# Four gelus in one ScalarE block, or in two blocks of two

## The chip, the core and the metric

The kernel runs on one core of one Trainium2 chip. The core has five engines with queues of their own, each of which works strictly in order: PE (TensorE, matmuls), DVE (VectorE), ACT (ScalarE), POOL (GpSimd) and SP (SyncE, which here only issues DMAs). They wait for one another through semaphores. The metric is device time in microseconds (us). The kernel before takes 3993.9 us, the median of 3 runs (3993.34 to 3994.86).

## What is computed

The input is x, 8 images of 384 channels and 32 x 32 places, so 1024 tokens each. Layer 0 is a two-way state space scan beside a small convolution, layer 1 is attention and a feed-forward part with quantised activations. Cut to what matters:

```python
# layer 0
fwd = mamba(x_flat, ...); bwd = flip(mamba(flip(x_flat), ...))
#   mamba: in-projection, 4-tap convolution, silu, softplus, then for each token
#   h = exp(delta * A) * h + delta * u * B;  y = sum over 16 states of h * C
local = sigmoid(depthwise_3x3(x_norm)) * x_norm
x = x + res_scale * (scale_mod * (fwd + bwd) + local)
# layer 1
t = t + attention(layernorm(t))          # 6 heads, causal
h = layernorm(t) @ sign(W1 - mean) + b1  # 1536 wide
h = gelu(clip(h * 128 / max|h|))         # the maximum over one image
t = t + clip((h @ sign(W2 - mean) + b2) * 128 / max)
```

The reference quantises in five groups of images, and with eight images each group is one image. The three images beyond them get zero from the feed-forward part, so it runs for five of the eight images only.

## The kernel before

Everything is float32, with channels on the 128 partitions and tokens along the free dimension. The weights' signs, the scan's inputs and other intermediate results go through DRAM.

**The planner.** The kernel's functions do not issue instructions. They record operations (`Op`), and `Plan.place` (line 246) then lays them out in time: it simulates the five engines with a cost for each operation (`Plan.cost`, line 221; a table load counts 2.8 there), gives each free engine the ready operation of the lowest rank, and hands out tile buffers on the way. `Plan.emit` (line 357) issues the result, which is why nearly every row of the profile has line 367. A rank is the operation's number in the order of recording. `hurry(offset)` lowers it, so that the operation goes ahead of others that are ready. `together()` makes one operation out of several instructions, between which nothing else of that engine can stand. A change in one place can move operations everywhere behind it.

**The order of recording.** The functions hand their steps to lists with a weight each (`Steps.of`). `spread_over` (line 1512) mixes lists by these weights. In the main loop (lines 1586 to 1613) the attention of an image is followed by its feed-forward part, mixed with `before_scan` of the image that comes three later; in that mix a step whose weight is a `Gap` counts `SHORT` (3.0) instead, all times `JOINT` (0.6). The scan units of the next image are spread over all of it.

**The scan.** There are 768 scan units, 96 for an image. One unit (`s_first`, `s_scan`, `s_sum`, lines 997 to 1045) is a chain over four engines:

1. POOL multiplies delta * u by B into a tile `scan_g` (128x1024), the first multiplication. There are 6 buffers of `scan_g`.
2. ACT makes two exps into PSUM, `ps_da` (two buffers).
3. DVE runs two scans over `scan_g`, each with one `ps_da`.
4. In half of the units ACT copies the last column out, the carry copy (`scan_carry<-scan_g`).
5. POOL multiplies `scan_g` by C in place, the second multiplication. It overwrites what the carry copy reads, so it waits for it.
6. For each pair of units PE gathers the states into `ps_y` (four small matmuls), which frees two `scan_g` buffers. The seed (`ps_y<-scan_us`, ACT) fills `ps_y` before the first gather, and `scan_yt<-ps_y` empties it in between.

These operations are recorded with a hurry of 600.

**The feed-forward part** (`feed_forward`, line 1394): a layernorm; 24 matmul groups with W1, evacuated by ACT into four tiles `st["h", q]` (128x3072, `big_big`); `quant_scale` (line 1382: a maximum on DVE, a transpose on PE with `small_col`, another maximum, add and multiply, reciprocal) which gives `st["s1"]`; then the gelus over the four tiles in place, with that scale, and four clamps on DVE; then six matmul groups of 12 with W2 (lines 1448 to 1478), whose k runs over the four tiles in turn, and each load of W2 is one of `mid_mid`; a second `quant_scale`; and the output.

**Beside it** runs `before_scan` (line 649). Its pieces that are named later: the taps of the 3x3 convolution (`local`, line 732: 8 multiply-adds on DVE for each of two halves, so 16, into PSUM, with `big_big` and `const_vec`), the gates block (`gates`, line 860: three silus of 128x1024, two tanhs of 128x512 and a table load back, one `together` group with a hurry of 60), `project_parts` (line 754, matmuls with `wx`), and `deltas` (line 913: matmuls with `wdt`, then the softplus block, three softplus and a table load, one `together` group).

**Tables.** ACT holds one table of functions. The set `LOG_EXP` (exp, ln, copies) is the resting one, and each group that needs another ends with `preload_act_table_set(LOG_EXP)`; the load ahead of the group is put in by the compiler. So every such group costs two loads.

After the feed-forward part comes the next image's attention: the output projection (`wout`), a layernorm (`onesc`), Q and K (`big_big` by `big_big`), V (`wv`), then the softmax.

Of the kernel before, what the change touches and what calls it, by code (L numbers as in the profile page):

```python
# [12 lines left out]
AF = mybir.ActivationFunctionType  # L13
ALU = mybir.AluOpType
# [7 lines left out]
NC = C // P  # L22
# [9 lines left out]
NF = FF // P  # L32
# [3 lines left out]
QCLIP = QMAX - QEPS  # L36
# [15 lines left out]
LOG_EXP = "natural_log_exp_and_others"  # L52
# [108 lines left out]
class Plan:  # L161
# [15 lines left out]
    @contextmanager  # L177
    def together(self):
        self.group = []
        yield  # L180
        self.group = None

    @contextmanager
    def hurry(self, offset):
        self.sooner += offset
        yield
        self.sooner -= offset
# [193 lines left out]
def kernel(  # L381
# [21 lines left out]
    nc = plan = Plan(tc, homes)  # L403
    together, hurry = plan.together, plan.hurry
# [989 lines left out]
    def feed_forward(b, t, emit):  # L1394
        st = {}

        @emit
        def _():
            st["xn"] = t()
            st["mxh"] = small.tile([P, NF], F32, name=f"mxh_{b}", tag="mxh", bufs=1)  # L1400
            st["mxy"] = small.tile([P, NC], F32, name=f"mxy_{b}", tag="mxy", bufs=1)
# [33 lines left out]
            st["s1"] = quant_scale(st["mxh"], f"h_{b}")  # L1435


        @emit.of(Gap(16.0))
        def _():
            with hurry(offset=60):  # L1440
                with together():
                    for q in range(NF // NC):
                        nc.scalar.activation(st["h", q], st["h", q], AF.Gelu, scale=st["s1"])
                    nc.scalar.preload_act_table_set(LOG_EXP)
                for q in range(NF // NC):
                    nc.vector.tensor_scalar(st["h", q], st["h", q], QCLIP, None, ALU.min)

        for m in range(NC):
            for h in range(NH):
# [220 lines left out]
```

## Time and profile before

| what | value |
|---|---|
| median of 3 runs | 3993.9 us |
| the profiled execution | 3992.03 us |
| its span, first to last instruction | 3990.2 us |
| mean granted TensorE clock | 0.901 |
| DMA | 612 MB, 153 GB/s over the span |
| scan exps, 1536 of 128x512 | 690 ns each |
| scans on DVE, 768 and 768 of 128x512 | 1267 and 1207 ns each |
| clamps, 20 of 128x3072 | 2325 ns each |
| taps on DVE, 128x496 | 732 ns each |
| silus of 128x1024, tanhs of 128x512 | 1046 and 644 ns each |

The five feed-forward parts' gelus begin at 1010.5, 1556.9, 2100.0, 2631.1 and 3156.2 us of the span. They are called blocks 1 to 5 below.

A row of a group shows line, engine, operation, output tile and input tiles without buffer numbers, shapes and count; then the total busy time, the mean of one in ns, and behind the second bar the time that the engine stood idle just before these instructions, with what ended it. A matmul of the program shows as two records. Busy times of matmuls are modelled at their ends, and so a PE that is busy is not at its peak.

### The profile page before, as it was taken

How to read it: one execution, taken by the hardware profiler on the slowest of the kernel's cores; microseconds unless marked ns; L12 is line 12 of the kernel's file. 1: busy time of each engine (PE TensorE's matmuls, PEld its weight loads, DVE VectorE, ACT ScalarE, POOL GpSimd, SP SyncE). 2: the span in 40 equal slices, each digit the busy share in tenths (PEclk: the TensorE clock that was granted, in tenths of full speed). 3: DMA queues.
4: the chain of work that ended last, by engine and by line, in shares of the span. 5: the costliest groups of instructions: out<-in, count | busy, mean ns of one | idle time of the engine just before them, and what ended most of it. 6: DMA issues, size and time to landing. Idle time of an engine off the chain costs nothing. (4 is left out here: it accounts for less than half of the span.)

```text
span 3990.2 us, 43097 instructions
## 1 busy us (share of the span) xinstructions
PE 3390.6 (85%) x12428; PEld 1334.1 (33%) x12428; DVE 3197.7 (80%) x4481; ACT 2627.6 (66%) x5114; POOL 3574.2 (90%) x1559
## 2 busy tenths in 40 slices
PE   5585779897799896998987989879989699898999
PEld 1131224332234332333322433323433234333344
DVE  5898987789878799788897688986779967878743
ACT  5767676866747777558677387674776746847635
POOL 2999999999999999999998799988999879999910
PEclk8695879999799997899987999979999799999999
DMA  7547664235543344742346433366334473333300
GB/s 246 195 157 247 230 239 133 90 132 186 194 170 123 117 157 149 250 151 93 127 162 224 157 122 113 130 202 237 104 111 136 157 252 128 111 123 114 121 14 32
DMA packets 338967, 612.01 MB, mean 153 GB/s; under 512 B 34616, under 2 KB 93416, under 8 KB 338728
## 3 DMA queue, kind: packets, MB, share of 16 engines
q1 hardware_dynamic: 329072, 593.10, 44.1%
q10 hardware_dynamic: 9656, 16.15, 1.2%
q8 instruction: 98, 1.61, 0.2%
q14 instruction: 141, 1.16, 0.1%
HBM read 456.03 MB, written 153.09 MB: 153 GB/s over the span
## 5 line engine op out<-in xcount | busy, mean ns | idle before, releaser
L367 POOL TENSOR_TENSOR scan_g<-scan_ud,scan_bc 128x1024 f32<-128x1024 f32 x768 | 1822.5, 2377 | 126.4 <-DMA scan_ud<-dram_sp_ud 62.6
L367 POOL TENSOR_TENSOR scan_g<-scan_g,scan_bc 128x1024 f32<-128x1024 f32 x768 | 1820.0, 2373 | 101.2 <-ACT scan_carry L367 55.5
L367 ACT ACTIVATE ps_da<-scan_dl,const_amat 128x512 f32<-128x512 f32 x1536 | 1053.4, 690 | 710.0 <-DVE scan_g L367 696.9
L367 DVE TENSOR_TENSOR_SCAN scan_g<-ps_da,scan_carry,scan_g 128x512 f32<-128x512 f32 x768 | 940.3, 1267 | 143.4 <-POOL scan_g L367 108.8
L367 PE MATMUL ps_any<-big_big,mid_mid 128*128 128x512 f32 x2016 | 956.8, 626 | 88.1 <-DVE big_big L367 64.8
L367 DVE TENSOR_TENSOR_SCAN scan_g<-ps_da,scan_g 128x512 f32<-128x512 f32 x768 | 895.9, 1207 | 153.7 <-POOL scan_g L367 98.3
L367 PE MATMUL ps_y<-scan_g,const_gather 128*32 128x512 f32 x3072 | 463.1, 679 | 236.7 <-POOL scan_g L367 232.3
L367 PEld LDWEIGHTS ps_any<-big_big,mid_mid 128*128 128x128 f32 x2016 | 389.0, 199 | 673.9 <-issue 491.1
L367 PE MATMUL ps_any<-big_big,big_big 128*128 128x512 f32 (+4 forms) x1728 | 548.0, 559 | 14.4 <-DVE big_big L367 5.6
L367 PE MATMUL ps_any<-const_ident,mid_mid 128*128 128x128 f32 x1728 | 311.5, 306 | 76.7 <-ACT mid_mid L367 45.3
L367 DVE CUSTOM_DVE_ANT_0 mid_mid<-ps_any,const_cmask 128x512 f32<-128x512 f32 (+3 forms) x576 | 292.0, 547 | 72.0 <-PE ps_any L367 71.6
L367 PEld LDWEIGHTS ps_any<-big_big,big_big 64*128 64x128 f32 (+1 forms) x1728 | 224.3, 191 | 303.1 <-issue 206.9
L367 DVE SCALAR_TENSOR_TENSOR ps_any<-big_big,const_vec,ps_any 128x496 f32<-128x496 f32 (+6 forms) x420 | 303.0, 727 | 16.4 <-ACT ps_any L367 6.6
L367 PEld LDWEIGHTS ps_any<-const_ident,mid_mid 128*128 128x128 f32 x1728 | 199.8, 150 | 309.3 <-issue 94.6
L367 ACT COPY ptp_ptn<-ps_any 128x512 f32<-128x512 f32 (+3 forms) x576 | 256.2, 479 | 49.0 <-PE ps_any L367 41.8
L367 PE MATMUL ps_any<-ptp_ptn,big_big 128*64 128x512 f32 (+3 forms) x1152 | 263.3, 537 | 13.8 <-ACT ptp_ptn L367 12.8
L367 ACT ACTIVATE mid_mid<-mid_mid,small_low 128x512 f32<-128x512 f32 (+3 forms) x384 | 242.5, 634 | 46.9 <-DVE small_low L367 46.6
L367 PEld LDWEIGHTS ps_y<-scan_g,const_gather 128*32 128x32 f32 x3072 | 63.2, 113 | 515.0 <-POOL scan_g L367 413.8
L367 ACT ACT_TABLE_LOAD x131 | 168.1, 1283 | 2.9 <-PEq L1657 0.7
L367 PE MATMUL ps_any<-mid_mid,const_onesc 128*128 128x512 f32 x252 | 130.2, 651 | 42.7 <-ACT mid_mid L367 27.5
L367 PE MATMUL ps_any<-mid_mid,const_wdt 25*128 25x512 f32 x192 | 139.0, 891 | 29.8 <-DVE mid_mid L367 15.9
L367 ACT COPY mid_mid<-ps_any 128x512 f32<-128x512 f32 x234 | 130.0, 584 | 35.9 <-PE ps_any L367 31.3
(102 smaller groups left out, 3136.3 us busy)
## 6 DMA issues: line engine op xcount, KB each, us to landing
scan_dl<-dram_sp_dl SPq DMA_DIRECT2D x384, 256.0 KB, 3.3
scan_ud<-dram_sp_ud SPq DMA_DIRECT2D x384, 256.0 KB, 3.9
scan_bc<-dram_rows SPq DMA_DIRECT2D x256, 256.0 KB, 3.4
scan_us<-dram_sp_u SPq DMA_DIRECT2D x96, 256.0 KB, 2.9
mid_mid<-dram_sp_u SPq DMA_DIRECT2D x96, 256.0 KB, 5.0
dram_sp_dl<-mid_mid SPq DMA_DIRECT2D x96, 256.0 KB, 4.6
dram_sp_ud<-mid_mid SPq DMA_DIRECT2D x96, 256.0 KB, 4.9
dram_sp_u<-mid_mid SPq DMA_DIRECT2D x42, 512.0 KB, 4.9
```

What stands on the lines that cost most here:

```text
L367: getattr(engine, what)(*[mapped(v) for v in args], **{k: mapped(v) for k, v in kwargs.items()})
```

## The change

The gelus of one feed-forward part are recorded as two steps, each with a group of two gelus and a load of the resting table, and with the two clamps that belong to them. The weights of the steps are 8 and 8 instead of 16 in the mix with `before_scan`; as each is a `Gap`, they count 3.0 each in the main loop, where one step counted 3.0 before.

```diff
-        @emit.of(Gap(16.0))
-        def _():
-            with hurry(offset=60):
-                with together():
-                    for q in range(NF // NC):
-                        nc.scalar.activation(st["h", q], st["h", q], AF.Gelu, scale=st["s1"])
-                    nc.scalar.preload_act_table_set(LOG_EXP)
-                for q in range(NF // NC):
-                    nc.vector.tensor_scalar(st["h", q], st["h", q], QCLIP, None, ALU.min)
+        for q0 in range(0, NF // NC, 2):
+
+            @emit.of(Gap(8.0))
+            def _(q0=q0):
+                with hurry(offset=60):
+                    with together():
+                        for q in range(q0, q0 + 2):
+                            nc.scalar.activation(st["h", q], st["h", q], AF.Gelu, scale=st["s1"])
+                        nc.scalar.preload_act_table_set(LOG_EXP)
+                    for q in range(q0, q0 + 2):
+                        nc.vector.tensor_scalar(st["h", q], st["h", q], QCLIP, None, ALU.min)
```

`NF // NC` is 4. The rest of the code is the same. The order in which the planner puts the instructions of all engines differs from a little ahead of the first gelu block on.

## The prediction

> **What bounds the kernel now.** The page's totals and its 40 slices come first, then its groups.
>
> ```profile
> PE 3390.6 (85%) x12428; PEld 1334.1 (33%) x12428; DVE 3197.7 (80%) x4481; ACT 2627.6 (66%) x5114; POOL 3574.2 (90%) x1559
> POOL 2999999999999999999998799988999879999910
> L367 POOL TENSOR_TENSOR scan_g<-scan_ud,scan_bc 128x1024 f32<-128x1024 f32 x768 | 1822.5, 2377 | 126.4 <-DMA scan_ud<-dram_sp_ud 62.6 <-PE ps_y L367 55.7 <-issue 8.0
> L367 POOL TENSOR_TENSOR scan_g<-scan_g,scan_bc 128x1024 f32<-128x1024 f32 x768 | 1820.0, 2373 | 101.2 <-ACT scan_carry L367 55.5 <-DVE scan_g L367 40.6 <-POOL scan_g L367 1.9
> L367 ACT ACT_TABLE_LOAD x131 | 168.1, 1283 | 2.9 <-PEq L1657 0.7
> L367 ACT ACTIVATE big_big<-big_big,small_qs 128x3072 f32<-128x3072 f32 x20 | 55.5, 2844 | 0.1
> ```
>
> POOL is full from the second slice to the 38th: each of 768 scan units takes two multiplications, 2.38 + 2.37 us. The chain of waits covers only the tail after POOL's last instruction (3% of the span), so it says nothing here. What matters is where POOL pauses: idle 126.4 + 101.2 us, of which 62.6 is the start, and most of the rest lies in stretches that begin at a block of gelus. Slices 22 and 23, 27 and 28, 32 and 33 (about 100 us each) show three of them. I then read the five blocks (tables loaded at 1009.2, 1555.6, 2098.7, 2629.8, 3154.9) in the timeline. The third:
>
> ```profile
> 2098.71 1.28 ACT L367 ACT_TABLE_LOAD   x1
> 2100.00 11.09 ACT L367 ACTIVATE big_big<-big_big,small_qs 128x3072 f32<-128x3072 f32 x4
> 2111.11 2.57 ACT L367 ACT_TABLE_LOAD   x2
> 2117.77 1.28 ACT L367 ACT_TABLE_LOAD   x1
> ...
> 2106.94 6.99 POOL L367 TENSOR_TENSOR scan_g<-scan_ud,scan_bc 128x1024 f32<-128x1024 f32 x3
> 2123.60 4.78 POOL L367 TENSOR_TENSOR scan_g<-scan_g,scan_bc 128x1024 f32<-128x1024 f32 x2 [9.66 <-DVE scan_g L367]
> ...
> 2101.67 9.83 DVE L367 SCALAR_TENSOR_TENSOR ps_any<-big_big,const_vec,ps_any 128x496 f32<-128x496 f32 x13
> 2111.41 9.14 DVE L367 TENSOR_SCALAR big_big<-big_big 128x3072 f32<-128x3072 f32 x4
> ...
> 2115.60 12.28 PE L367 MATMUL ps_any<-big_big,mid_mid 128*128 128x512 f32 x24 [11.25 <-DVE big_big L367]
> 2192.74 20.87 PE L367 MATMUL ps_any<-big_big,mid_mid 128*128 128x512 f32 x48
> 2214.72 13.94 POOL L367 TENSOR_TENSOR scan_g<-scan_ud,scan_bc 128x1024 f32<-128x1024 f32 x6 [7.57 <-PE ps_y L367]
> ...
> 2090.00:2310.00 220.00, 193.90 (x566) 76.88 (x568) 163.31 (x208) 120.93 (x198) 177.82 (x78) 0.88 0.56 189
> ```
>
> Each timeline line is start, length, engine, operation, tiles. The gelus and the gates block (silus, tanhs) behind them hold ACT from 2098.71 to 2119.05 with no scan exp between. POOL runs out of scanned tiles at 2113.94 and loses 9.66 us. PE waits too: the clamp that feeds the second weight matrix's matmuls (W2) stands on DVE behind 13 convolution taps. From 2115.60 to about 2300 PE hardly stops, and POOL pauses because its tiles are not gathered: 7.57 us behind 24 matmuls (48 records, 0.87 us a matmul). In the last line (window, then busy PE, PEld, DVE, ACT, POOL) PE is busier than POOL. So blocks 3 to 5 are bound by ACT for 10 us, then by PE. In blocks 1 and 2 PE isn't full; POOL loses 3.88 + 2.17 and 4.07 + 2.52 us there.
>
> **The change, part by part.** The gelus (20 x 2844 ns), the 20 clamps and all DMAs stay in number and size. Added are ten table loads, two in each of five blocks: 10 x 1283 ns = 12.8 us of ACT, which has 34% of the span free. A block of 1.28 + 11.10 + 1.28 = 13.7 us becomes two of 1.28 + 5.55 + 1.28 = 8.1. What stands between them is in the order of the changed program, read against the order before:
>
> - Blocks 1 and 2: one scan unit (a carry copy, two exps) between the halves and one between the second half and the gates.
> - Block 3: only a 0.6 us copy, then a seed of y. Block 4: nothing. Block 5: the gates come between the halves, and a softplus block that stood 8 units after the gelus now stands one unit after them.
>
> So ACT's longest stretch without a scan exp falls from 13.7 to 8.1 us in blocks 1 and 2, and grows in the others: 20.4 to 24.1 us (block 3: two loads 2.6, and the copy and the seed, which stood ahead), 20.4 to 22.9 (4 and 5).
>
> Block 1: the halves start about one unit earlier, since the quantiser's reciprocal no longer stands behind a scan pair on DVE. One unit is scanned 5 us later, the next 0.8 earlier: 8.1 + 1.5 + 8.1 + 1.5 + 6.7 = 25.9 us against 13.7 + 1.5 + 6.7 = 21.9 started about 4.7 later. Bounds: -3.9 (its first stall gone) and +2.6 (two loads on the path). I take -1, near the middle.
> Block 2: likewise, and three clamps (7.22 us) no longer stand together ahead of the scans at 1583.75. Bounds -6.6 and +2.6; I take -2.
> Block 3: on DVE the first clamp now stands ahead of the last four taps, so W2 may start 4 x 0.73 = 2.9 us sooner. Counted in PE's order over the 16 pairs of gathers behind the gelus, six V matmuls (0.66 us each) move out of them: 4.0 us less ahead of POOL. Against that, POOL's next scanned tile comes 2.6 us later; the gather that wants it is reached by PE some 1.4 us after that, so most of the delay is covered by PE's matmuls. Without this cover it costs up to 3.7. Bounds -6.9 and +3.7; I take -5.
> Block 4: three taps, 2.2 us, and one V matmul, 0.7. Scans 2.6 us later, covered by about 1.5 us. Bounds -2.9 and +2.6; I take -3, on the PE side, since PE is the bound there for 180 us.
> Block 5: no tap moves, PE's work ahead of POOL is the same over these pairs. Two clamps and two sums now stand ahead of a scan, and the softplus (4.3 us) comes early. Bounds 0 (hidden, as PE is busy from 3171.8) and 2.6 + 4.3 = +6.9; I take +3.
>
> Sum: -1 - 2 - 5 - 3 + 3 = -8 us; of the bounds, -20.3 and +18.4. Behind each block the planner orders other work anew; between these stretches POOL idles only 2 to 5 us in 310 to 430, so little is to be won there. The profiled run took 3992.03 us (3990.2 of span, 1.8 around), 1.9 under the median; its span should come to 3982 and the median to 3993.9 - 8 = 3986 us.
>
> The row of the loads shows 1283 ns, and the gelu begins 0.01 us after. The Trainium skill (ScalarE: Activation LUTs, What ACT_TABLE_LOAD costs) gives the same load and a drain of some 1380 ns with each switch; by it ten switches would be an estimated 26.6 us, not 12.8, and with all of them on the path 4020, not 4007. The trace shows no such gap behind a load.
>
> **Rivals.**
>
> *The loads are paid on the path (slower).* Three of the five splits have no scan between the halves, so the stall of 9.66 us in block 3 (8.79 and 5.36 in 4 and 5) grows by the loads. If POOL's tile at the end of the gates comes later than PE reaches its gather, PE stops as well, and the earlier W2 start is worth nothing. It decides from 1.4 us of lateness. Price: all ten loads, 12.8 us, 4007 us. For it: 20.4 to 24.1 us on ACT. Against: PE's 11 us wait at that place is for DVE, not ACT. The rule in the Trainium skill (ScalarE: Activation LUTs, Rules for kernel authors) to group by table set before switching speaks for this case.
>
> *The long matmul runs break up (much faster).* In the changed order the longest runs of W2 matmuls between two gathers are 21, 15 and 17 where they were 24, 29 and 34. The stalls behind them were 7.57, 7.72 and 10.17. Three matmuls less give back 2.6, and in blocks 4 and 5 the whole, 7.7 + 10.2: 20 us, 3974 us. Against: PE has as much to do altogether, and other runs grow (the 20 us run of block 5 behind the output projection).
>
> *Nothing moves (same).* POOL's gap only changes place: later scans in blocks 3 to 5 against fewer waits in 1 and 2; 3994 us.
>
> That the change does not do what it says is part of the first: in block 4 two table loads stand back to back between the halves.
>
> **How the numbers follow.** A measurement here tells about 0.2%, 8 us, from no change. The forecast gets 0.42 (0.22 beyond -8, 0.17 within, 0.03 slower), the loads on the path 0.33 (0.31 slower, 0.02 within), the broken runs 0.14, nothing 0.11 (all within). Faster 0.36, same 0.30, slower 0.34. The likeliest case's own range is 3979 to 3994. Together the range is 3973 (all lower bounds) to 4010, just under all upper bounds.
>
> **What would show it.** 141 table loads. In blocks 1 and 2 POOL's idle time near the gelus falls below 6.0 and 6.6 us. In block 3 W2 starts some 16 us after the first load or sooner, POOL's wait right at the gates is 11 to 13 us, and the idle time after it is shorter by more than that grows. In block 5 the first three second multiplications are spread wider by about 4 us. I am wrong if PE waits for POOL right after W2 starts, if POOL's idle time between 2090 and 2310 grows beyond today's 42 us, or if the attention stages, where POOL hardly stops now, begin to show pauses.

## The result, and the profile after

The changed kernel takes 3983.99 us (median of 9 runs, 3981.79 to 3985.73). The kernel before took 3994.34 us beside it (9 runs, 3990.76 to 3999.45). The ratio is 0.9974, with a 95% interval from 0.9966 to 0.9982: 10.4 us less, 0.26%. The profiled execution took 3981.79 us and its span is 3979.9 us, 10.3 less than before.

From the page of the changed kernel: the busy totals, POOL's 40 slices, POOL's two groups and the table loads.

```profile
PE 3393.5 (85%) x12428; PEld 1334.4 (34%) x12428; DVE 3196.9 (80%) x4483; ACT 2639.9 (66%) x5122; POOL 3577.6 (90%) x1559
POOL 2999999999999999999997899989999798999910
L367 POOL TENSOR_TENSOR scan_g<-scan_ud,scan_bc 128x1024 f32<-128x1024 f32 x768 | 1825.9, 2381 | 115.2 <-DMA scan_ud<-dram_sp_ud 62.8
L367 POOL TENSOR_TENSOR scan_g<-scan_g,scan_bc 128x1024 f32<-128x1024 f32 x768 | 1821.7, 2375 | 95.6 <-ACT scan_carry L367 71.8
L367 ACT ACT_TABLE_LOAD x141 | 180.9, 1283 | 3.1 <-PEq L1659 0.7
```

The ten loads are there (131 became 141, 12.8 us), and ACT is busy 12.3 us longer. POOL makes the same multiplications, and its idle time fell from 126.4 + 101.2 to 115.2 + 95.6 us, so by 16.8; but the two groups are busy 5.1 us longer (the last section shows how a multiplication can stretch). Its pauses still lie about the blocks, at slices 22, 23, 27, 32 and 34.

The third block in the timeline of the changed kernel (start, length, engine, operation, tiles, count, idle time before):

```profile
2092.11 1.28 ACT L367 ACT_TABLE_LOAD   x1
...
2093.41 5.60 ACT L367 ACTIVATE big_big<-big_big,small_qs 128x3072 f32<-128x3072 f32 x2
...
2099.48 2.34 POOL L367 TENSOR_TENSOR scan_g<-scan_ud,scan_bc 128x1024 f32<-128x1024 f32 x1
...
2102.22 5.60 ACT L367 ACTIVATE big_big<-big_big,small_qs 128x3072 f32<-128x3072 f32 x2
2102.74 3.42 DVE L367 TENSOR_SCALAR big_big<-big_big 128x3072 f32<-128x3072 f32 x2
2104.54 7.99 PE L367 MATMUL ps_any<-big_big,mid_mid 128*128 128x512 f32 x12 [14.64 <-DVE big_big L367]
...
2112.47 1.06 PE L367 MATMUL ps_y<-scan_g,const_gather 128*32 128x512 f32 x8
...
2113.71 4.66 POOL L367 TENSOR_TENSOR scan_g<-scan_ud,scan_bc 128x1024 f32<-128x1024 f32 x2 [11.89 <-PE ps_y L367]
```

W2 now starts 12.4 us after the first load (2104.54 against 2092.11); it was 16.9. POOL's pause at the gates grew from 9.66 to 11.89 us. What came after it shrank. The 7.57 us behind the long W2 run are gone; within the run (21 matmuls now) POOL pauses 2.80 us, and within the output projection 4.12 us, where it was 1.72. The pauses behind Q, K and V went from 3.44 + 7.34 + 2.99 to 5.47. The window from 2090 to 2310 us of the changed kernel shows the sum (busy us of PE, PEld, DVE, ACT, POOL):

```profile
2090.00:2310.00 220.00, 198.81 (x617) 78.66 (x617) 166.57 (x221) 131.34 (x221) 184.17 (x81) 0.91 0.57 193
```

POOL is idle 35.8 us in it, where it was 42.2.

To place gains I use 48 marks: the copies `scan_yt<-ps_y` on ACT, one for every 16 scan units. Six of them lie in smooth stretches between the blocks (the 12th, 19th, 26th, 33rd, 40th and 48th, at 766.7, 1489.2, 1983.5, 2508.6, 3028.7 and 3590.2 us in the kernel before). How much sooner or later a kernel reaches them gives the share of each stretch. For the changed kernel: +0.8 up to the first, then -3.0 (block 1), -4.0 (2), -7.8 (3), -0.1 (4), +1.7 (5), and +2.0 to the end of the span. These come from one execution of each kernel, and stretches with the same instructions in the same order still differ by up to 1, so only steps beyond that are read.

### The profile page after: what moved, and what is told of

Read it like the earlier page. It is cut to its first block, busy times and chain, and to the rows that moved or that the text cites. A ratio compares the mean times of both kernels' runs of the same rounds, so it can differ in the third digit from the quotient of the medians.

```text
span 3979.9 us, 43074 instructions
## 1 busy us (share of the span) xinstructions
PE 3393.5 (85%) x12428; PEld 1334.4 (34%) x12428; DVE 3196.9 (80%) x4483; ACT 2639.9 (66%) x5122; POOL 3577.6 (90%) x1559
## 3 DMA queue, kind: packets, MB, share of 16 engines
q8 instruction: 98, 1.61, 0.2%
## 5 line engine op out<-in xcount | busy, mean ns | idle before, releaser
L367 POOL TENSOR_TENSOR scan_g<-scan_ud,scan_bc 128x1024 f32<-128x1024 f32 x768 | 1825.9, 2381 | 115.2 <-DMA scan_ud<-dram_sp_ud 62.8
L367 POOL TENSOR_TENSOR scan_g<-scan_g,scan_bc 128x1024 f32<-128x1024 f32 x768 | 1821.7, 2375 | 95.6 <-ACT scan_carry L367 71.8
L367 PE MATMUL ps_any<-ptp_ptn,big_big 128*64 128x512 f32 (+3 forms) x1152 | 265.5, 541 | 14.6 <-ACT ptp_ptn L367 13.6
L367 ACT ACT_TABLE_LOAD x141 | 180.9, 1283 | 3.1 <-PEq L1659 0.7
L367 PE MATMUL ps_any<-mid_mid,const_wdt 25*128 25x512 f32 x192 | 134.7, 871 | 33.2 <-DVE mid_mid L367 16.7
L367 DVE COPY big_big<-ps_any 128x512 f32<-128x512 f32 (+1 forms) x85 | 53.8, 633 | 132.4 <-PE ps_any L367 132.1
```

Source lines behind the costliest of these rows:

```text
L367: getattr(engine, what)(*[mapped(v) for v in args], **{k: mapped(v) for k, v in kwargs.items()})
```

## The experiments

All times below are medians, beside runs of the kernel before on the same chip (3993.9 us in the first and third group, 3994.6 in the second). The first expectations speak of a gain by POOL's progress. That count misjoined some rows in blocks 4 and 5; the marks, each a single instruction, replace its +2.7 and +2.4 by -0.1 and +1.7.

### Splitting only some of the images

```diff
-        for q0 in range(0, NF // NC, 2):
+        nq = 2 if b in ORDER[:2] else 4      # split_01; split_234: b in ORDER[2:]
+        for q0 in range(0, NF // NC, nq):
...
-            @emit.of(Gap(8.0))
+            @emit.of(Gap(4.0 * nq))
```

> The feed-forward parts of images 0 and 1 are split as in the changed kernel, those of images 2, 3 and 4 keep one block of four gelus. POOL's progress (the time at which it begins its n-th multiplication) gained 3.0 us on the kernel before at the first block of the changed kernel, 3.7 at the second, 7.7 at the third, and lost 2.7 and 2.4 at the fourth and fifth. Theory A (each split acts in its own stretch; in the first two the gain is that ACT can make scan exps between the halves): the first two gains stay, 3994 - 6.7 = 3987 us, and the progress shows nothing of its own at blocks 3 to 5. Theory B (the gain is the earlier start of the matmuls with W2, so of the later blocks): some 3993 us. Theory C (the planner's new order behind the change decides, and the places of gain are chance): gains and losses of several us turn up at blocks 3 to 5 although they are as before.

> The reverse: images 2, 3 and 4 are split, 0 and 1 keep one block of four. Theory A: -7.7 + 2.7 + 2.4 = -2.6 and up to 1.7 at the end, 3990 to 3992 us, and POOL's progress up to 2000 us is that of the kernel before. Theory B: most of the gain of the changed kernel, 3986 us. Theory C: the sizes at blocks 3 to 5 are others than in the changed kernel, by more than 3 us at each.

With images 0 and 1 split: 3983.91 us (11 runs), ratio 0.9977 [0.9969, 0.9986], as fast as the changed kernel. With images 2 to 4 split: 3997.38 us (11 runs), 1.0007 [0.9998, 1.0016], no gain. The first keeps the gains of its split blocks, 2.8 and 2.9 us. But most of its change lies where it isn't split: block 3, which has its four gelus in one block as before, gained 12.5 us, and blocks 4 and 5 lost 5.3 and 2.8. In the second kernel the halves of block 3 stand on ACT as in the changed kernel, with loads and one copy between, and W2 starts 12.7 us after the first load, nearly as early as in the changed kernel (12.4), yet the block gains 1.1 instead of 7.8. What differs is around them: the seed of `ps_y` comes behind the gates, not ahead of them (POOL's pause there is 16.68 us, not 11.89), and 18 V matmuls stand between two gathers, not 14. So the time in blocks 3 to 5 does not follow from how they are split. Theory C, the order, was the only one of the three that both runs allow.

### The loads alone, newly planned

```diff
                     for q in range(NF // NC):
+                        if q == 2:
+                            nc.scalar.preload_act_table_set(LOG_EXP)
                         nc.scalar.activation(st["h", q], st["h", q], AF.Gelu, scale=st["s1"])
```

> The four gelus stay one block, with a table load to and from between the second and third: the ten loads of the changed kernel without a place for other work. Theory A: the 2.6 us are on POOL's path in blocks 1 and 2, where ACT's block ends its wait (+2.6 each), and in 3 to 5 half covered by PE's long runs (+1.2 each, by the 1.4 us of cover in the prediction): +9, 4003 us. Theory D (all loads paid): +12.8, 4007 us. Theory E (ACT has 34% of its time free, the loads are hidden): 3994 us.

4008.5 us (5 runs), 1.0038 [1.0025, 1.0051]: +14.6, more than all ten loads (12.8). Theory D is nearest, but the stretches don't fit it: +5.5, +2.5, +8.2, +2.2, 0.0, where two loads are 2.6 each. The planner had made a new order here too, so this run couldn't price the loads.

### Clamps behind their own gelus

```diff
+        if what == "activation" and self.group:
+            op.done_at[id(written[0].tile)] = op.time
...
-                [b.end + (0.0 if b.name == op.name and not b.dma else self.SIGNAL) for b in op.before.values()],
+                [
+                    b.start + b.done_at[id(op.tiles[0])] + self.SIGNAL
+                    if op.parts[0][0] == "tensor_scalar" and id(op.tiles[0]) in b.done_at
+                    else b.end + (0.0 if b.name == op.name and not b.dma else self.SIGNAL)
+                    for b in op.before.values()
+                ],
```

> No split and no added load: four gelus in one block, but the planner is told when each gelu of the block ends, so that each clamp may be placed behind its own gelu and not behind the whole block. On DVE the clamps now stand one by one among the last taps of the convolution, and the gates block on ACT moves some 3 to 9 exps back. Theory B (W2's earlier start is what helps in blocks 3 to 5): W2 starts 5 to 8 us sooner there, the long runs of W2 matmuls between gathers shorten, and the gates' silus no longer stand right behind the gelus: -7 at block 3 and 0 to -5 at 4 and 5, 3982 to 3988 us. Theory A alone (ACT's block of four is what POOL waits for): blocks 1 and 2 as before, little in 3 to 5, 3992 to 3995 us. The other side: the taps that the clamps push back hold the gates and so the next image's convolution; +3, 3997 us.

4043.65 us (4 runs), 1.0125 [1.011, 1.0141]: +50, against every theory, with +16.7 in block 2, +8.6 in block 3 and +22.3 in block 4. The timeline of this kernel in block 2 shows a large part of it, DVE and POOL side by side:

```profile
1567.69 13.01 DVE L375 TENSOR_SCALAR big_big<-big_big 128x3072 f32<-128x3072 f32 x2
1568.11 2.39 POOL L375 TENSOR_TENSOR scan_g<-scan_ud,scan_bc 128x1024 f32<-128x1024 f32 x1
1570.43 2.38 POOL L375 TENSOR_TENSOR scan_g<-scan_g,scan_bc 128x1024 f32<-128x1024 f32 x1
1572.75 4.67 POOL L375 TENSOR_TENSOR scan_g<-scan_ud,scan_bc 128x1024 f32<-128x1024 f32 x2
...
1579.09 3.78 PE L375 MATMUL ps_any<-big_big,mid_mid 128*128 128x512 f32 x4 [13.54 <-DVE big_big L375]
...
1584.51 2.35 POOL L375 TENSOR_TENSOR scan_g<-scan_ud,scan_bc 128x1024 f32<-128x1024 f32 x1 [7.09 <-issue]
...
1593.12 7.12 POOL L375 TENSOR_TENSOR scan_g<-scan_g,scan_bc 128x1024 f32<-128x1024 f32 x3 [6.27 <-DVE scan_g L375]
```

Two clamps take 13.01 us. The first doesn't get through while POOL's multiplications run back to back; the W2 matmul that waits for it starts at 1579.09, 1.67 us after POOL's run ends (1572.75 + 4.67 = 1577.42). POOL then stands 7.09 us; the times point to PE's gather, which stands behind those matmuls and ends at 1584.34, 0.17 us before POOL goes on. DVE works in order, so it makes no scans meanwhile, and POOL stands 6.27 us more for lack of scanned tiles. An earlier clamp meets a full POOL; it stops DVE, and through DVE and PE it stops POOL. All clamps of this kernel by tile (minimum, median and maximum in ns, first and last start):

```profile
L375 DVE TENSOR_SCALAR big_big<-big_big x20: 1727/2757/11345, 1016.4 to 3220.5; 128x3072 f32<-128x3072 f32 x20
```

The same instruction takes 1.73 us or 11.35. W2 did start sooner after the first load, by 6.3 us in block 3 and 9.0 in block 5, and neither block gained. So theory B fell, and a term appeared that none of the theories had: where the clamps stand against POOL's runs. The planner's order is new here too, so not all of the 50 us need come from the clamps.

### The same split under other plans

One number of the planner was changed, in the kernel with four gelus and in the split one. No instruction is added by it.

```diff
         if what == "preload_act_table_set":
-            return 2.8
+            return 2.2          # four_22 and split_22; 1.4 in four_14 and split_14
```

> The kernel before, with one number of the planner changed: it counts 2.2 for a table load where it counted 2.8. No instruction is added or removed; the planner orders them a little otherwise everywhere. With its partner (the same number in the split kernel) it asks whether the gain of the split lasts under another order. Theory F (blocks 3 to 5 are a matter of the order that happens to come out): this kernel already lies up to 8 us to either side of 3994, most of it at the blocks of images 2 to 4, though nothing was split. Theory G (the order matters little, the split brings the gain): 3992 to 3996 us.

> The split kernel with the planner's 2.2 for a table load; blocks 1 and 2 come out in the same order on ScalarE as in the split kernel. Theory F: against its partner with four gelus 5 to 7 us are gained at blocks 1 and 2 together, as in the changed kernel and in the one that splits only images 0 and 1, and the blocks 3 to 5 come out anywhere between -12 and +8 in sum. Theory G: 8 to 12 us faster than its partner, with most of the gain at the same places as in the changed kernel, 7 to 8 of it in block 3.

> As the first of these, with 1.4 for a table load, near the 1.28 that one load takes. Theory F: within 8 us of 3994 on either side, by another sum over the blocks than with 2.2. Theory G: 3992 to 3996 us.

> The split kernel with 1.4 for a table load. Here the gates block of images 3 and 4 (the next images' convolution beside blocks 1 and 2) comes much later, ten exps or more behind the gelus, as it did in the kernel with early clamps. Theory F: the gain at block 1 stays, -3; at the second the late gates cost several us as they did with early clamps (+17 there), and the rest is open: 3985 to 4010. Theory G: 8 to 12 us faster than its partner.

| planner's price of a load | four gelus | ratio to before | two and two | ratio to before |
|---|---|---|---|---|
| 2.8 | 3994.34 | | 3983.99 | 0.9974 [0.9966, 0.9982] |
| 2.2 | 3982.8 | 0.9971 [0.9960, 0.9981] | 3994.57 | 1.0001 [0.9992, 1.0010] |
| 1.4 | 4011.2 | 1.0046 [1.0032, 1.0059] | 4041.13 | 1.0119 [1.0105, 1.0132] |

The kernel with four gelus under another plan is as fast as the changed one, with nothing split. Under that plan the split costs 3994.57 - 3982.8 = 11.8 us, under the third 29.9. Theory G fell. Theory F was right that the order alone moves the time, but its sizes were too small: the kernels with four gelus moved by -11.8 and +16.6 us where it allowed 8 either way, blocks 3 to 5 together gave +12.0 with 2.2 where it allowed up to +8, and the split kernel with 1.4 took 4041 us where it said 3985 to 4010. The price of a load also moves work ahead of the first block (with 1.4 both kernels are 24 us late at the first mark). And theory F's own claim, that blocks 1 and 2 gain 5 to 7 in any case, fell too: split less unsplit is -1.1 and +1.7 there with 2.2, and +2.8 and -0.9 with 1.4.

### Split and order taken apart

In the last group the planner runs as it did, and the blocks are changed only when its result is issued. PE, DVE, POOL and SP keep the same instructions in the same order.

```diff
-            for op in self.place():
+            for op in self.merged(self.place()):
...
+    def merged(self, ops):      # the second half's gelus join the first
+                    first.parts = first.parts[:-1] + op.parts
+                    op.parts, first = [], None
...
+    def halves(self, ops):      # the second half behind three more ACT operations, or ahead of its first user or the gates
+                if mine or since == 3 or (op.name == "scalar" and len(op.parts) > 4):
+                    yield rest
...
+    def inside(self, ops):      # a load to and from in the middle
+                op.parts = op.parts[:2] + op.parts[-1:] + op.parts[2:]
```

> The changed kernel with its order kept as planned on every engine, but with the two halves of each gelu block put together again when the instructions are issued: four gelus and one table load back stand where the first half stood, and the place of the second half is empty. PE, DVE, POOL and SP have the same instructions in the same order as the changed kernel; ten table loads are gone. Theory F (the gain of the changed kernel is the order that the planner happened to make): it stays at 3984 us or gains up to the ten loads on top, 3974 to 3986 us, with -7 to -8 in the stage of block 3. Theory A (it is the split): the gains in blocks 1 and 2 go (+6 to +7), 3989 to 3994 us.

> The reverse: the kernel before with its order kept on PE, DVE, POOL and SP, and only the gelu block split when the instructions are issued. In blocks 1 and 2 a carry copy and two exps (or a seed, a copy and an exp) come between the halves, with table loads around; in blocks 3 to 5 the gates follow too closely, so the second half stands right behind the first with two loads between. Theory A: -3 in each of blocks 1 and 2, 0 to +2.6 in each of the others: 3988 to 3996 us. Theory F: no gain at any block, since the loads are paid where ACT is waited for (+5.5 and +2.6 were measured with the loads in one block): 3997 to 4005 us.

> The kernel before in its own order, with a load to and from in the middle of each block of four: the loads alone, without any new order. The kernel with the loads in its own newly planned order took +14.6. Theory F and theory D (all loads paid): +8 to +13, 4002 to 4007 us, by +2.6 for each block whose gelus POOL waits for. Theory E (hidden): 3994 to 3997 us. What lies between this and the run before it is worth of the place between the halves alone.

The stretches of one execution each, in us against the kernel before:

| kernel | median us (runs) | ratio | to block 1 | 1 | 2 | 3 | 4 | 5 | end |
|---|---|---|---|---|---|---|---|---|---|
| changed | 3983.99 (9) | 0.9974 | +0.8 | -3.0 | -4.0 | -7.8 | -0.1 | +1.7 | +2.0 |
| its order, four together | 3988.93 (11) | 0.9991 [0.9982, 1.0000] | +0.8 | +0.5 | +0.4 | -9.2 | 0.0 | +1.9 | +2.1 |
| order of before, split | 3996.8 (11) | 1.0012 [1.0004, 1.0021] | +1.0 | -0.1 | +0.1 | 0.0 | +2.9 | +0.4 | -0.1 |
| order of before, loads only | 4000.87 (11) | 1.0020 [1.0011, 1.0029] | +0.8 | +3.3 | +0.1 | 0.0 | +3.0 | +0.5 | -0.1 |

The first two rows differ from each other only by the gelu blocks, and so do the last two and the kernel before; this settles most of it. In the changed kernel's order, halves instead of one block are worth about 5 us by the medians (3988.93 to 3983.99), 7 in the executions of the stretches: -3.5 in block 1, -4.4 in block 2, +1.4 in block 3, and -0.2 in 4 and in 5. Block 3's gain belongs to the order: -9.2 with four gelus together. In the order of before the same split costs 2.9 us, and the loads alone cost 7.0: they are paid in blocks 1 and 4 (3.3 and 3.0, where two loads are 2.6) and hidden in 2, 3 and 5. The place between the halves is thus worth the 3.4 us of block 1 there, just what its loads cost. Both theories were half right: theory A in blocks 1 and 2 of the changed order, theory F in block 3 and in the order of before.

Why block 1 gains in one order and not in the other is seen in POOL's pauses there. First the changed kernel's order with four together, then the changed kernel, then the kernel before, then its order with the split:

```profile
1019.21 2.34 POOL L383 TENSOR_TENSOR scan_g<-scan_g,scan_bc 128x1024 f32<-128x1024 f32 x1 [7.65 <-ACT scan_carry L383]
...
1035.11 4.91 POOL L383 TENSOR_TENSOR scan_g<-scan_ud,scan_bc 128x1024 f32<-128x1024 f32 x2 [1.30 <-PE ps_y L383]
```

```profile
1013.68 2.35 POOL L367 TENSOR_TENSOR scan_g<-scan_g,scan_bc 128x1024 f32<-128x1024 f32 x1 [2.15 <-ACT scan_carry L367]
...
1031.77 4.66 POOL L367 TENSOR_TENSOR scan_g<-scan_ud,scan_bc 128x1024 f32<-128x1024 f32 x2 [1.87 <-PE ps_y L367]
```

```profile
1023.21 2.34 POOL L367 TENSOR_TENSOR scan_g<-scan_g,scan_bc 128x1024 f32<-128x1024 f32 x1 [3.88 <-ACT scan_carry L367]
1027.72 7.79 POOL L367 TENSOR_TENSOR scan_g<-scan_ud,scan_bc 128x1024 f32<-128x1024 f32 x2 [2.17 <-PE ps_y L367]
```

```profile
1020.22 2.34 POOL L386 TENSOR_TENSOR scan_g<-scan_g,scan_bc 128x1024 f32<-128x1024 f32 x1
1021.12 3.06 DVE L386 TENSOR_SCALAR big_big<-big_big 128x3072 f32<-128x3072 f32 x1
...
1024.23 2.07 PE L386 MATMUL ps_any<-big_big,mid_mid 128*128 128x512 f32 x2 [13.55 <-DVE big_big L386]
1026.24 1.82 PE L386 MATMUL ps_y<-scan_g,const_gather 128*32 128x512 f32 x8
...
1028.25 7.54 POOL L386 TENSOR_TENSOR scan_g<-scan_ud,scan_bc 128x1024 f32<-128x1024 f32 x2 [5.69 <-PE ps_y L386]
```

One block of four leaves POOL waiting 7.65 us for a carry copy that stands behind it on ACT. In halves the copy and two exps come in between, and the pause is 2.15. In the order of before the split also removes the pause at the carry copy (3.88), but a pause of 5.69 comes in place of 3.88 + 2.17, and ACT doesn't end it. In that order POOL has made its three first multiplications ahead of this second one (from 1013.29 on), and its next needs a tile that PE's gather frees. The gather stands on PE behind a W2 matmul, which waits for the first clamp, and the clamp stands on DVE behind ten taps and takes 3.06 us beside POOL. In the changed order three first multiplications stand behind the second one (from 1015.99 on), so POOL can use at once what the earlier carry copy gives it. In block 2 of the order of before POOL waits 4.07 us, with the split as without, for scans that stand on DVE behind the first clamp (4.87 and 4.88 us). So what the split is worth hangs on how PE, DVE and POOL are ordered around it.

### A nudge to the plan

```diff
+                    plan.dearer = 1.4 if b in ORDER[:2] else 0.0
                     nc.scalar.preload_act_table_set(LOG_EXP)
+                    plan.dearer = 0.0
```

with `return 2.8 + self.dearer` in the planner's price of a load.

> The kernel before with the planner counting 4.2 instead of 2.8 for the table load behind the gelus of images 0 and 1 alone. No instruction is added, removed or changed, and about 120 of PE's 4802 listed rows stand elsewhere. Theory F: 2 to 8 us to one side or the other. Theory G (the order matters little): 3993 to 3996 us.

4004.57 us (7 runs), 1.0028 [1.0018, 1.0039]: +10.7, beyond even theory F's 8, and 8.1 of the profiled 12.5 lie in block 3, whose own price was not touched. Its timeline there, DVE's clamps and POOL:

```profile
2115.50 9.29 POOL L368 TENSOR_TENSOR scan_g<-scan_ud,scan_bc 128x1024 f32<-128x1024 f32 x4
2119.03 12.39 DVE L368 TENSOR_SCALAR big_big<-big_big 128x3072 f32<-128x3072 f32 x4
...
2134.46 2.35 POOL L368 TENSOR_TENSOR scan_g<-scan_g,scan_bc 128x1024 f32<-128x1024 f32 x1 [9.67 <-DVE scan_g L368]
```

The first clamp is issued while POOL has most of four multiplications ahead. It takes 7.38 us and ends at 2126.4, 1.6 us behind POOL's run; the other three follow at 1.67. In the kernel before the first clamp of block 3 takes 4.14 us (2111.41 to 2115.55, POOL's run ends at 2113.93). In the changed kernel POOL had run dry 0.9 us before the clamp, and two take 3.42. The held clamp isn't shown to cause the loss, though: POOL's pause at the gates is 9.67 us, where the kernel before has 9.66, and what is new are pauses of 2.05, 2.65 and 2.36 us behind it. The kernel with the loads newly planned has the same order on PE here (484 of 484 records up to 2310 us) and nearly the same pauses, so its +8.2 in this block isn't the price of its loads.

## Why the prediction was right, and where it was not

The forecast was 3986 us, the likeliest case -8 with its own range 3979 to 3994. The time is 3983.99. The direction and the sum came out; the reason given for them holds in part.

- **Block 1 (-1) and block 2 (-2).** Measured -3.0 and -4.0, mis-sized but inside their bounds. The stated sign, POOL's pause falling below 6.0 and 6.6 us, was seen: 2.15 + 1.87 and 1.56 + 1.28. The mechanism is shown by the two kernels that share the changed order: halves are worth 3.5 and 4.4 us there. It doesn't hold in every order; in the order of before, with a scan unit or a like piece between the halves too, it came to -0.1 and +0.1. Against the kernel before, block 1 also has a new pause of 2.41 us ahead of the gelus (997.62) and no longer one of 3.20 behind them (1120.88), which the working didn't have.
- **Block 3 (-5).** Measured -7.8, beyond its bound of -6.9. It is the order, as -9.2 with the split taken out shows; the working took the order of DVE and PE into its sum, but booked it to the split. And W2's earlier start, its first term, doesn't bring the gain. It was put at 2.9 us of taps and came 4.5 sooner relative to the first load (the working lacked POOL's hold on the clamp, 2.4 of the 4.14 us that the first clamp took before). With images 2 to 4 split it came 4.2 sooner and the block gained 1.1; with images 0 and 1 split it came 1.2 sooner and the block gained 12.5. The V matmuls that move, its second term, don't suffice either: the split kernel with 1.4 in the planner has the same 14 V matmuls between two gathers and lost 10.6 us here. What goes with the gain in all profiles is a place that the working didn't name. In the six that gain 6 us or more, PE makes its first gather behind 6 or 7 W2 matmuls (`x12` above, as a matmul is two records); in the other eight it makes it behind 10 to 15, and those lie between -1.1 and +10.6. It wasn't tried to move this gather alone. The sign of being wrong, PE waiting for POOL behind the start of W2, didn't show: up to 2300 us no such wait is over 0.3 us, before or after.
- **The cover of the loads.** In the changed order halves cost 1.4 us in block 3, near the 1.2 that a cover of 1.4 leaves of two loads, and nothing in blocks 4 and 5 (-0.2 each). In the order of before they cost 0.0, 2.9 and 0.4: the cover, too, is one of the order.
- **Block 4 (-3).** Measured -0.1; this step failed. W2's longest run fell from 29 matmuls to 15, and its pause of 7.72 us went (1.36 behind the run after it), but the pause at the gates rose from 8.79 to 11.80, with 2.66 behind it, and one of 3.04 stands in the output projection. Most of the gain was given back at the block itself. It isn't the loads: with four gelus together the block comes to 0.0.
- **Block 5 (+3).** Measured +1.7. The late scans are there: the first three second multiplications lie 16.8 us apart instead of 10.4, 6.4 wider where about 4 was said, and pauses of 14.38 and 7.24 us stand where 5.36, 1.00 and 3.60 stood. The shorter W2 runs behind them (17 matmuls at most between two gathers; the pause of 10.17 is gone) took back most. With four gelus together the block comes to +1.9, so this too is the order's.
- **Begin and end.** +0.8 and +2.0 had no term.
- **The sum.** That it came within 2 us or so is luck in part: blocks 1 to 3 came out 2.0, 2.0 and 2.8 us better than said, block 4 2.9 worse, block 5 1.3 better, and 2.8 at begin and end were left out.
- **Rival one, the loads on the path.** It had 0.33, and in the order of before it is half true: 7.0 of 12.8 us. The Trainium skill's rule (ScalarE: Activation LUTs, Rules for kernel authors) to group by table set holds there; in the changed kernel's order the ungrouped halves are 5 us faster.
- **Rival two, the runs that break up.** The runs did shorten, and 20 us did not come back, since the pauses at the gates grew. What it names is again of the order: with four gelus together the same later pauses are there (4.11 and 5.45 us where the changed kernel has 4.12 and 5.47).
- **The third rival, nothing moves.** It fails: the kernel moved, and over the three plans split less unsplit is -10.4, +11.8 and +29.9 us, so the plan decides even the sign.

The step that failed as a whole is "Behind each block the planner orders other work anew; between these stretches POOL idles only 2 to 5 us in 310 to 430, so little is to be won there." It is true of the stretches between. It hid that the new order at the blocks themselves moves the time by 10 us or more either way, with or without a split.

What stays open: which instructions' places make the order good. Over the 14 kernels profiled here the total time of the 20 clamps (36.6 to 69.9 us busy) goes with the time from the first mark to the last (correlation 0.95, and 0.81 without the two slowest), but it wasn't tried to free the clamps from POOL with all else kept, nor to move one gather. No version here is told apart from the changed kernel as faster; the one with four gelus and 2.2 in the planner (3982.8 us) equals it with ten loads fewer.

## What to carry to other kernels

Where a planner lays out the whole program, one edit gives one sample of its order: a nudge that changed no instruction cost 10.7 us here, as much as the edit seemed to gain. So hold the order fixed and change the edit alone, or compare the edit under several plans, before a gain under 0.3% is put down to it. And a split of a block on an in-order engine paid here where the engine that it released had more work that it could do at once, and not where the next piece waited for a third engine.

## What was not expected of the hardware

The clamp, a DVE TENSOR_SCALAR of 128x3072 from and to SBUF, took from 1.73 to 11.35 us with the same operands. In the 14 profiles 86 clamps took over 1.9 us, and each of them ended 1.61 or 1.62 us after a POOL multiplication had ended. Where the clamp got in first, POOL's multiplication stretched instead, from 2.37 to 3.78 us at 1576.16 in the kernel before, behind a clamp that began at 1576.01. The scans and taps, which read or write PSUM on DVE, show no such stretch: 1.17 to 1.29 and 0.67 to 0.76 us in all 14. The Trainium skill (SBUF — State Buffer, Who interferes with whom) says that VectorE and GpSimd share a port pair, that a `tensor_scalar` can run in a mode that needs it, and that the one that issues second is blocked until the first finishes. The trace agrees that one blocks the other wholly. It differs on how long: four multiplications that POOL began after the clamp's recorded start (1568.11 to 1577.42, against 1567.69) all went ahead of it. The ten added loads took 1283 ns each as the others did, and each of the ten groups of gelus began 0.01 us behind its load.
